# A two-layer graph network on one core: where the weight loads and the weight preparation stand among the operations of the first graphs

## The chip, the cores and the metric

The kernel runs on one core of a Trainium2 chip. The metric is the device time of one execution, in microseconds (us), as the median of several runs. A core has five engines, each with its own stream of instructions that it takes strictly in program order: PE (matrix multiply, with its weight loads shown as PEld), DVE (VectorE), ACT (ScalarE), POOL (GpSimd) and SP (SyncE), which here issues every transfer (DMA) between memory and the core. An engine that meets an instruction whose input is not there waits, and everything behind it on that engine waits too.

## What is computed

There are 64 graphs of 256 nodes with 256 features, and an adjacency matrix for each. Each graph goes through two layers:

```python
# layer 0: attention over 8 heads, with a value matrix chosen by the edge type
q, k = src @ Wq + bq, src @ Wk + bk
attn = softmax(q @ k.T / sqrt(dh))
out = sum over r of (attn * (adj == r)) @ (src @ Wv[r] + bv[r])
x = ln(src + out @ Wo + bo)                    # gain g1, shift beta1
x = ln(x + gelu(x @ W1 + b1) @ W2 + b2)        # gain g2, shift beta2
# layer 1: two graph attentions, then a feed-forward
h = gat(gat(x, adj, W1, a1), adj, W2, a2)      # the layer's own W1, W2
h = ln(x + h)
y = ln(h + relu(h @ w_ff1 + b_ff1) @ w_ff2 + b_ff2)
```

The weights are the same for all graphs. They are loaded once, and some are changed once before use (see below).

## The kernel before

**One plan, sorted.** The kernel writes its order out by hand. Each graph is an object whose `operations()` (line 697) gives 210 named operations: `xT` transposes the input on DVE, `qk0` and `qk1` are the query and key products on PE, `s0` and `s1` the scores, `maxmh`, `expmh`, `recmh`, `nrmmh` the softmax of head h in half m, `eTmh` its transpose in 32x32 squares on DVE, `eWmh` and `eRmh` the two transfers that finish that transpose by way of memory, `pmmh` the product with the mask, `po0` and `po1` the products with the values, `vp1` to `vp7` the value products and `va..` their sums, `wo` the output product; then the first feed-forward (`a..`, tiles ffa), the two graph attentions (`ga..`, `z..`, `h1..`, `h2`), the second feed-forward (`b..`, tiles ffb) and `store`. `load` brings in the input x (`xin`, four transfers) and the adjacency (`adi`) of one graph, `y` the input once more as a residual.

`PLACES` (line 29) gives each operation a number, its place. Operation n of graph g has the place `g * PERIOD + PLACES[n]` with `PERIOD` = 46.8, so some five graphs are under way at once. Places are only sorted; they are not waited for. The sorted list is the program order of all five engines:

```python
plan = [(t, len(PLACES), lambda i=i: nc.sync.dma_start(*loads[i])) for i, t in enumerate(LOAD_PLACES)]
for place, f in (
        (V_PLACE, v_weights),
        (OUT_PLACE, out_bias),
...
    plan.append((place, len(PLACES), f))
for g in range(B):
...
    plan += [(g * PERIOD + t, i, ops[n]) for i, (n, t) in enumerate(PLACES.items())]
with tc.manual_schedule():
    for _, _, f in sorted(plan, key=lambda p: p[:2]):
        f()
```

**Ahead of the plan** (lines 190 to 210) SP issues the input of graph 0 (`xin` in four transfers, `adi`), `wq`, `wk`, `bq_c`, `bk_c`, four blocks of `wv`, two rows of `bv_r` and `bv_c`, and DVE scales the query bias (`bqs_c`, line 210).

**In the plan** stand, beside the operations, 49 weight loads (`LOAD_PLACES`, in the order in which the list `loads` is filled, lines 213 to 239; the trace puts them all at line 791) and six steps that run once:

- `v_weights` (line 267), at `V_PLACE`: nine DVE instructions on `wv` and `bv_r`, which make the seven combined value matrices that `vp1` to `vp7` use.
- `out_bias` (line 275), at `OUT_PLACE`: four matmuls of `bv_c` with `wo` on PE (tile `bo_ps`), then one DVE addition into `bo_r`, which `yb` adds to the residual.
- `ffn_weights` (line 241), at `FFA_PLACE` for `w1`, `w2` and at `FFB_PLACE` for `f1`, `f2`: 32 matmuls with one output column on PE (line 247), two scalings of 128x1024 on ACT (line 251), and on DVE one small addition, one of 128x256 and four of 128x512 (lines 249, 252, 261 to 264).
- `gat_weights` (line 282), at `GAT_PLACE`: transposes and products on PE with DVE copies between them, each waiting for the one before (lines 289, 290, 297, 299, 304, 306), ending in `gext`, which `ga0` and `ga1` use.
- `any_odd` at `ODD_PLACE`, after the last graph's checks.

With the places before, the sorted list begins with 13 loads, `v_weights`, seven loads, `out_bias`, and 21 more loads. Only then come `te` of graph 0, one more load, and the first operations of graph 0: `xT`, `qk0`, `qkc0`, `chk`. The load of `bo_r`, which `out_bias` adds to, is the eighteenth of the plan's loads. The other seven loads are part 0 of `f1` behind the input load of graph 1, then `gl1_r`, a part of `gw1`, `bf2_r`, `bl2_r`, `be2_r` and `g2_r`, one at a time, among the operations of graphs 0 to 2. `ffn_weights` for `f1` stands just ahead of `xS` of graph 1 and the one for `w1` just ahead of `s1` of graph 1.

Of the kernel before, what the change touches and what calls it, by code (L numbers as in the profile page):

```python
# [63 lines left out]
    "rt4": 345.1762, "nb4": 348.7424, "ln4": 355.9706, "lg4": 361.3841, "lb4": 362.9841, "store": 364.6106,  # L64
}
LOAD_PLACES = [
    -1614.873, -876.860, -2013.345, -937.005, -414.952, -1429.108, -1287.906, -564.689, -101.489, -232.236, -554.653,
    -886.559, -645.093, -1037.230, -879.521, -1583.499, -310.508, -761.901, -160.300, 256.504, 211.016, -1033.278,
    -110.148, -55.769, 172.714, -816.528, -200.307, -634.823, -786.173, -139.875, 168.880, -731.757, 150.912,
    -640.846, -119.211, -981.427, -22.481, -1384.415, -1320.156, -1310.193, -716.722, -1407.675, -1020.008, 74.666,  # L70
    -646.340, -542.109, 179.232, -895.390, 197.294,
]
V_PLACE, OUT_PLACE, FFA_PLACE, GAT_PLACE, FFB_PLACE, ODD_PLACE = -942.888, -786.173, 197.294, 224.563, 183.686, 240.000

# [971 lines left out]
```

## Time and profile before

| What | us |
|---|---|
| median of 3 runs | 3197.49 |
| lowest and highest of the runs | 3196.38, 3198.89 |
| the profiled execution's own time | 3196.43 |
| its span in the trace | 3194.6 |
| span from 140 to 3040: PE busy, of 2900 | 2867.19 |
| DVE busy there | 2234.91 |
| ACT busy there | 2192.56 |
| POOL busy there | 2077.52 |
| first 25 us of the span: PE busy | 2.07 |

The span is the trace's time from the first to the last instruction; the execution's own time is 1.8 us longer. From 140 us on PE is busy 99% of the time and the others 72% to 77%. The profile gives, for each stretch of time, the busy time of each engine and the granted clock of PE (1.00 is full speed, 0.50 half). Transfers are told by their issue on SP; the median time from issue to landing was 3.1 us for a part of `xin`, 3.0 us for an `eW`, 3.5 us for an `eR`, 3.5 us for `bo_r` and 7.4 us for the 1 MB of `w2`. A load's issue on SP took 0.42 to 0.69 us, mostly 0.60.

### The profile page before, as it was taken

To read this page: it belongs to the slowest core of one execution; us is meant where nothing else is said; L and a number is where in the kernel's file an instruction comes from. 1 tells how busy PE (TensorE), PEld (TensorE's weight loads), DVE (VectorE), ACT (ScalarE), POOL (GpSimd) and SP (SyncE) were. 2 spreads that over 40 slices of the span, in tenths; PEclk is the share of its full clock that TensorE was granted. 3 is DMA by queue.
4 is the path that set the end of the run, shared out by engine and by line. 5 is a ranking of instruction groups with operands and counts; after the bars stand their busy time and mean duration, and the time that the engine had idled before them with its cause. 6 is when DMAs were issued, how large, how long until landed. Compare 5 with 4: busy or idle time off the path is not lost. (4 is left out here: it accounts for less than half of the span.)

```text
span 3194.6 us, 63709 instructions
## 1 busy us (share of the span) xinstructions
PE 3075.6 (96%) x21725; PEld 2586.6 (81%) x21725; DVE 2374.0 (74%) x5153; ACT 2325.6 (73%) x6599; POOL 2193.0 (69%) x2630
## 2 busy tenths in 40 slices
PE   6899999999999999999999999999999999999995
PEld 4688888888888888888888888888888888888774
DVE  5777777777777777777877877877777777777742
ACT  5677777777777777777777777777777777777742
POOL 1476776776776676676676676676677677677664
PEclk8999999999999999999999999999999999999997
DMA  6554455455455455455455455455455455455421
GB/s 194 148 151 144 141 154 146 139 154 149 138 152 150 140 149 152 140 148 154 137 150 154 136 151 154 137 151 153 136 151 152 137 151 151 138 153 150 133 70 31
DMA packets 808331, 456.62 MB, mean 143 GB/s; under 512 B 334528, under 2 KB 717376, under 8 KB 808000
## 3 DMA queue, kind: packets, MB, share of 16 engines
q1 hardware_dynamic: 808000, 452.49, 49.0%
q8 instruction: 174, 2.85, 0.4%
q14 instruction: 157, 1.29, 0.1%
HBM read 242.63 MB, written 201.33 MB: 139 GB/s over the span
## 5 line engine op out<-in xcount | busy, mean ns | idle before, releaser
L568 ACT ACTIVATE e<-e,rden 128x256 f32<-128x256 f32 x1024 | 455.9, 505 | 86.2 <-DVE rden L563 86.0
L408 PE MATMUL ffb_ps<-ffb_T,f 128*128 128x256 f32 x2048 | 461.7, 384 | 25.8 <-DMA ffb_T<-ffb_T_d 23.5
L408 PE MATMUL ffa_ps<-ffa_T,w 128*128 128x256 f32 x2048 | 474.6, 380 | 0.0
L558 ACT ACTIVATE e<-s,nmax 128x256 f32<-128x256 f32 x1024 | 469.3, 469 | 6.8 <-DVE nmax L550 3.8
L408 PEld LDWEIGHTS ffb_ps<-ffb_T,f 128*128 128x128 f32 x2048 | 392.6, 193 | 85.3 <-DMA ffb_T<-ffb_T_d 20.5
L577 DVE TENSOR_TENSOR pm<-eT,adT 128x512 f32<-128x512 f32 x512 | 437.7, 856 | 0.0
L326 DVE STREAM_TRANSPOSE eT_sq<-e 128x512 f32<-128x512 f32 x512 | 350.9, 695 | 110.7 <-DMA ffa_T_d<-ffa_T_sq 98.1
L408 PEld LDWEIGHTS ffa_ps<-ffa_T,w 128*128 128x128 f32 x2048 | 380.7, 191 | 47.4 <-ACT ffa_h L416 0.2
L373 POOL TENSOR_SCALAR rs_x<-mv_x 128x2 f32<-128x2 f32 x256 | 56.6, 221 | 453.1 <-DVE mv_x L369 445.6
L550 DVE TENSOR_REDUCE nmax<-s 128x2 f32<-128x512 f32 x512 | 336.0, 667 | 7.3 <-PE s L545 7.2
L416 ACT ACTIVATE ffb_h<-ffb_ps,bf_c 128x256 f32<-128x256 f32 x512 | 215.0, 472 | 123.4 <-PE ffb_ps L408 123.4
L384 ACT ACTIVATE ffa_res<-ffa_res,nb_x,rs_x 128x256 f32<-128x256 f32 x256 | 139.4, 594 | 191.5 <-POOL nb_x L379 185.3
L644 DVE SCALAR_TENSOR_TENSOR ga_z<-ga_z 128x512 f32<-128x512 f32 x64 | 88.1, 1377 | 235.9 <-ACT ga_z L641 235.9
L431 POOL TENSOR_TENSOR ffa_t<-ffa_h,ffa_t 128x512 f32<-128x512 f32 x128 | 165.1, 1290 | 128.8 <-ACT spare L692 121.5
L431 POOL TENSOR_TENSOR ffb_t<-ffb_h,ffb_t 128x512 f32<-128x512 f32 x128 | 191.0, 1492 | 89.2 <-ACT ffb_h L416 89.2
L416 ACT ACTIVATE ffa_h<-ffa_ps,b_c 128x256 f32<-128x256 f32 x512 | 214.3, 472 | 51.9 <-PE ffa_ps L408 51.1
L644 DVE SCALAR_TENSOR_TENSOR gb_z<-gb_z 128x512 f32<-128x512 f32 x64 | 44.3, 692 | 226.8 <-ACT gb_z L641 226.8
L558 ACT ACTIVATION_READ_ACCUMULATOR e<-s,nmax 128x1 f32 x1024 | 209.5, 205 | 0.0
L374 POOL TENSOR_TENSOR rs_x<-rs_x,nhalf 128x2 f32<-128x2 f32 x256 | 181.8, 710 | 21.3
L530 DVE TENSOR_TENSOR v<-v,v_ps 128x256 f32<-128x256 f32 x448 | 169.2, 400 | 0.6 <-PE v_ps L521 0.6
L351 POOL TENSOR_TENSOR ffa_res<-ffa_res,g_r 128x512 f32<-128x512 f32 x64 | 81.7, 1276 | 122.2 <-ACT ffa_res L384 122.2
L545 PE MATMUL s<-kT,qT 32*128 32x256 f32 x2048 | 149.9, 404 | 4.7 <-ACT e L558 4.7
(163 smaller groups left out, 8016.0 us busy)
## 6 DMA issues: line engine op xcount, KB each, us to landing
eT_d<-eT_sq SPq DMA_DIRECT2D x512, 256.0 KB, 3.0
eT<-eT_d SPq DMA_DIRECT2D x512, 256.0 KB, 3.5
xin<-in_x_dram SPq DMA_DIRECT2D x256, 64.0 KB, 3.1
adi<-in_adj_dram SPq DMA_DIRECT2D x64, 256.0 KB, 2.8
y<-in_x_dram SPq DMA_DIRECT2D x64, 256.0 KB, 4.4
ffa_T_d<-ffa_T_sq SPq DMA_DIRECT2D x64, 256.0 KB, 2.5
ffa_T<-ffa_T_d SPq DMA_DIRECT2D x64, 256.0 KB, 3.0
hT_d<-hT_sq SPq DMA_DIRECT2D x64, 256.0 KB, 2.0
```

The source lines that it names most:

```text
L326: nc.vector.transpose(self.sq.rearrange("p a c k y -> p (c k) a y"), src.rearrange("p c (k a x) -> p (c k) a x", k=KD, a=A))
L374: nc.gpsimd.tensor_tensor(self.rs, self.rs, nhalf, ALU.pow)
L384: nc.scalar.activation(yc, yc, AF.Identity, bias=self.nb[:, c:c + 1], scale=self.rs[:, c:c + 1])
L408: nc.tensor.matmul(p[:, f - f0, :], self.wa[:, k, f * P:(f + 1) * P], self.x.nodes(k), start=(k == 0), stop=(k == KD - 1))
L416: nc.scalar.activation(self.h[half][:, f1 + f, :], self.ps[f0][:, f, :], self.func, bias=self.ba[:, f0 + f:f0 + f + 1])
L431: nc.gpsimd.tensor_tensor(out, a, b, ALU.subtract)
L530: nc.vector.tensor_tensor(self.v_part(*to), self.v_part(*src), self.ps["v", i], ALU.add)
L545: nc.tensor.matmul(self.s4[m][h][:, ic * N:(ic + 1) * N], self.qT[hp, m, ic * P:(ic + 1) * P], self.kT[hp, m, :], start=True, stop=True)
L550: nc.vector.tensor_reduce(self.nmax[m, h], self.s4[m][h].rearrange("p (c n) -> p c n", c=C), AX.X, ALU.max, negate=True)
L558: nc.scalar.activation(e[:, ic, :], self.s4[m][h][:, ic * N:(ic + 1) * N], AF.Exp, bias=self.nmax[m, h][:, ic:ic + 1], accum_out=self.den[ ...
L568: nc.scalar.activation(e[:, ic, :], e[:, ic, :], AF.Copy, scale=self.rden[m, h][:, ic:ic + 1])
L577: nc.vector.tensor_tensor(self.pm[m, h].rearrange("p c k (b y) -> p (c k) b y", b=A), t.rearrange("p b c k y -> p (c k) b y"), self.adT.re ...
```

## The change

Only numbers change: the 49 places of `LOAD_PLACES` and five of the six places of the steps that run once. `PLACES` and every function stay as they are, so the order of the graphs' own operations among each other is the same.

```diff
 LOAD_PLACES = [
-    -1614.873, -876.860, -2013.345, -937.005, -414.952, -1429.108, -1287.906, -564.689, -101.489, -232.236, -554.653,
...
+    101.366, 142.216, 210.928, 179.882, 111.464, 161.951, 112.848, 100.995, 176.282, 144.653, 176.020, 153.991,
+    122.933, 161.019, 117.691, 142.137, 176.282, 109.079, 176.294, 241.513, 253.083, 121.392, 182.287, 196.253,
+    207.821, 129.075, 215.004, 184.114, 158.647, 204.480, 111.464, 207.869, 213.180, 214.956, 213.949, 222.383,
+    259.685, 196.355, 250.874, 266.888, 159.287, 109.005, 208.310, 182.294, 221.373, 230.689, 234.043, 257.548,
+    184.117,
 ]
-V_PLACE, OUT_PLACE, FFA_PLACE, GAT_PLACE, FFB_PLACE, ODD_PLACE = -942.888, -786.173, 197.294, 224.563, 183.686, 240.000
+V_PLACE, OUT_PLACE, FFA_PLACE, GAT_PLACE, FFB_PLACE, ODD_PLACE = 113.801, 158.647, 184.117, 225.125, 272.083, 240.000
```

Sorted, the plan then runs as follows (gN. is an operation of graph N; operations between those named are left out):

```
g0.te, w1 part 3, wo, g0.load, g1.te, g0.xT, bl1_c part 0, w2, w1 part 0, gl1_r, w1 part 2, V_WEIGHTS,
g0.qk0, be1_c 1, g0.qkc0, g0.chk, gw1 0, g1_c 3, g0.qk1 ... g0.max01, gx ... be1_c 2, bo_r, g0.cast, g1_c 0, g0.eT00 ...
g1.load, g0.s1 ... g0.eW00, g1_c 2 ... g1.xT, g0.vp1 ... g0.eW03 ... a part of gx, OUT_BIAS, g0.vc1, gl1_c 3 ...
g0.vp6, g0.y, be1_c 0, g1.qk0, w1 part 1, g0.eR03, g0.jT, g0.eW01 ... g0.eW10 ... g0.eR00, g0.eT02 ...
g1_c 1, b1_c, be1_c 3, b2_r, g0.eW02 ... g0.eR01, be1_r ... gw1 1, bl1_c 2, a2c 1, bl2_r, FFN_WEIGHTS(w1), g1.xS, g0.eW12 ...
g0.eR02, g0.eW11 ... g0.pm00, gw1 2, gl1_c 0, g0.eR12, g2.load, g1.s1, g0.po0 ... g2.xT ... a part of gx ...
gw1 3, g1.y, bl1_r ... bl1_c 1, g1.eR03, g1.jT, g0.pm13, g1_r, g1.eW01 ... f1 0, f1 2 ... f1 1, a2c 0 ... g1.eW10 ...
bl1_c 3 ... g1.eR00 ... f1 3 ... g0.aW, g1.eW02, g2.exp01, g2.max03, g1.yb, GAT_WEIGHTS, g2.rec00 ...
g0.aR ... f2, g2.xS, g1.eW12, g0.au3 ... bf2_r ... g2_r ... gl1_c 1 ... be2_r ... gl2_r ... bf1_c ...
g0.hT ... gl1_c 2 ... g0.hW ... g0.hR ... g2.yb, FFN_WEIGHTS(f1), g0.ga1, g0.gac1, g0.ga0 ...
```

Fourteen loads now stand ahead of `g1.load` (42 before) and 35 behind it (seven before). `GAT_PLACE` moves past `g2.exp01`, `g2.max03` and `g1.yb`. `FFB_PLACE` moves from the operations of graph 1 to the first graph attention of graph 0, behind all loads.

## The prediction, made before the changed kernel was run

> **What bounds the kernel now.** I read the page first, for the bound and for where the bound fails to hold; then windows of ten microseconds over the start; then the order of time and the waits there.
>
> ```profile
> span 3194.6 us, 63709 instructions
> PE 3075.6 (96%) x21725; PEld 2586.6 (81%) x21725; DVE 2374.0 (74%) x5153; ACT 2325.6 (73%) x6599; POOL 2193.0 (69%) x2630
> PE   6899999999999999999999999999999999999995
> PEclk8999999999999999999999999999999999999997
> ```
>
> PE is full in all slices but the first two and the last, and its clock is full there. So the time is the filling, then PE's work at full speed, then the draining. The change leaves all instructions and, behind the steps it moves, their order; it can only shift the moment from which PE stays full. The windows (PE, PEld, DVE, ACT and POOL busy, PE's granted clock, DMA share, GB/s) find that moment:
>
> ```profile
> 0.00:10.00 10.00, 0.00 (x0) 0.00 (x0) 0.55 (x4) 1.69 (x3) 0.69 (x6) 1.00 0.64 158
> 10.00:20.00 10.00, 2.07 (x4) 1.17 (x4) 2.73 (x8) 0.00 (x0) 0.00 (x0) 1.00 0.57 158
> 60.00:70.00 10.00, 9.28 (x65) 5.91 (x65) 9.86 (x21) 9.96 (x19) 0.00 (x0) 0.60 0.88 240
> 120.00:130.00 10.00, 5.59 (x31) 3.98 (x30) 8.24 (x20) 6.35 (x21) 9.59 (x15) 0.80 0.51 136
> 140.00:150.00 10.00, 10.00 (x93) 7.69 (x94) 4.95 (x8) 8.22 (x23) 5.04 (x4) 1.00 0.45 131
> ```
>
> PE does nothing of the graphs for 25 us, then is held up, and is full from 140 on. Up to there every microsecond by which the order of work comes forward comes off the end; behind it only added PE work counts. The order of time (start, duration, instruction, idle time before it and its releaser) shows what holds the start:
>
> ```profile
> 8.87 0.17 DVE L210 TENSOR_SCALAR bqs_c<-bq_c 128x2 f32<-128x2 f32 x1 [7.98 <-DMA bq_c<-in_L_gnn_bq_dram]
> 20.36 0.58 SPq L791 DMA_DIRECT2D bo_r<-in_L_gnn_bo_dram  x1
> 23.90 0.42 DVE L280 TENSOR_TENSOR bo_r<-bo_ps,bo_r 128x256 f32<-128x256 f32 x1 [9.42 <-DMA bo_r<-in_L_gnn_bo_dram]
> 24.24 0.70 DVE L468 STREAM_TRANSPOSE xT<-xin 128x512 f32<-128x512 f32 x1
> 38.99 2.64 SPq L185 DMA_DIRECT2D xin<-in_x_dram  x4
> 43.46 0.71 DVE L468 STREAM_TRANSPOSE xT<-xin 128x512 f32<-128x512 f32 x1 [2.16 <-DMA xin<-in_x_dram]
> 53.21 3.63 PE L247 MATMUL ffb_b_ps<-bl_c,f 128*128 128x1 f32 x32
> 54.51 0.71 DVE L326 STREAM_TRANSPOSE eT_sq<-e 128x512 f32<-128x512 f32 x1 [2.31 <-DMA eT_d<-eT_sq]
> 56.70 6.04 PE L247 MATMUL ffa_b_ps<-be_c,w 128*128 128x1 f32 x32
> 127.81 3.80 PE L622 MATMUL ga_wps<-gext,hT 128*128 128x260 f32 x8 [4.41 <-DMA hT<-hT_d]
> ```
>
> The first transpose stands on DVE behind the addition of `out_bias`, which waits for `bo_r`, eighteenth load of the plan. The input of graph 1 goes out at 38.99, behind 42 loads. From 54.5 to 77 DVE never idles, so DVE sets the pace there, while PE runs 58 to 67 at half speed.
>
> **The change, part by part**, in time against the profiled execution (3196.43; its span and 1.8 around it).
>
> *Start.* `xT` now follows `bqs_c` on DVE, which ends at 9.04. `xin` was issued by 3.52, and the slowest of its transfers took 5.2, so it is there by 8.7; `wq` and `wk` (issued 4.22, 4.74, landing in 3.8, 3.9) by 8.6. So `xT` starts at 9.1 instead of 24.24: **-15.2**. `v_weights` (nine DVE instructions) goes behind it, still waits for `bv_r` until 12.46 and ends at 14.5; `chk` ends at 15.1, and the next DVE work, the first maximum, comes at 32.52 - 15.2 = 17.3. It costs nothing; without that cover, 3.5 (4x0.29, 0.43, 4x0.42, less overlap).
>
> *Graph 1's input.* Fourteen loads stand ahead of it: 9.75 + 14x0.6 = 18.2. One more delay shows in SP's waits: of `w2` (1 MB, issued 21.97, 7.4 to land) the eighth next load waited 2.0 until 29.4. `w2` now goes out at 11.9 and the eighth next, `be1_c` 2, waits until 19.3, by which the issue comes to about 20.6; landed, 20.6 + 2.64 + 3.1 = 26.3. DVE is ready for it at 41.3 - 15.2 = 26.1. The wait of 2.16 goes; what I keep is **-1.0** (between 0 and -2.2), since `out_bias` now takes its 2.07 on PE there, in a gap that was 1.74 wide.
>
> *SP ahead of DVE.* The wait of 2.31 at 54.51 is for an `eW` that SP issued late: at 43 SP was still at the loads, so `eR03` and the adjacency transposes ran late. SP now comes to `eW00` at 24 (19 earlier), six loads more use up some 3 of its 4 us lead, and four of the later ones lie where SP would wait for `eT02` anyhow: **-2.0** (0 to -3.4, with the 1.14 wait before it).
>
> *ffn_weights.* Both stood at 53 to 69; now that of `w1` alone stands where that of `f1` stood. DVE, which sets the pace, loses 0.12 + 0.40 + 4x0.69 = 3.3 us of work, in the row from 59.81 to 62.84: **-3.0** (0 to -3.6). ACT loses 2.2, PE 3.6 to 6.0, none on the path. Its last inputs are near: `be1_c` 3 lands at about 38, when PE arrives at 37 to 38; `be1_r` at 42.5, DVE at 42: within the next term.
>
> *SP with more loads.* Between `y` of graph 0 and the step 11 loads stand against three, between graph 2's input and `wo` nine against one. I carried SP's queue forward by rows: graph 2's input lands about 1.0 behind DVE, and `eR13` brings `pm13` 1.2 late: **+2.2**. Bounds: nothing, if SP's own waits (31 us in the first 320 for DVE's value sums alone) take them up; 28 loads x 0.6 = +16.8 if none does.
>
> *gat_weights.* Its first DVE copy (86.07) now stands behind one more maximum: **+0.7**, since PE and DVE take turns in it (0 to +0.7).
>
> *ffn_weights for f1, new place.* It falls into PE's gap of 4.41 ahead of `ga1`, waiting for `hT`: 32 matmuls at 113 ns are 3.6. ACT was idle 2.63 there (needs 2.3); DVE then waits 3.53 for `ga_z` (needs 3.3). Cover gone, it is PE's 3.6; I take **+0.5**. The 1 MB of `f2` (5.6 to land) goes ahead of `eW12`; what needs the next `eR` comes 8 us later, so nothing (up to +5.6).
>
> One rule speaks for more. The Trainium skill, TensorE: Matmul & The Clock Gate, section "Why this matters for your kernels", asks for no idle gap of over some 3 us, as the clock falls by half after it; the gap at 123.4 agrees (0.50 from 126 to 132), and by the rule filling it would keep the clock. But the row of 56.70 shows 32 such matmuls back to back, with the clock at 0.50 from 58 on: one-column matmuls did not hold it. So I take nothing for the clock, and leave the rule's result a rival.
>
> Sum: -15.2 - 1.0 - 2.0 - 3.0 + 2.2 + 0.7 + 0.5 = **-17.8**, so 3178.6 for an execution like the profiled one; the median lies 1.1 higher: **3179.7**.
>
> **The rivals.**
>
> *The filled gap keeps the clock.* `ga_wps` then takes 8x0.24 = 1.9 instead of 3.8 (0.24: half of 0.475), and the 0.5 falls away: 3177.3. Against it stands the row at 56.70. With the skill's page beside it I give it 0.12. It shares this end with the case that SP costs nothing.
>
> *The loads cost half of what they can.* SP is one queue, and each head needs an `eW` and an `eR` from it. For it: DVE's waits in the first 320 us for writes that SP had issued late (7.1 on `ffa_T`, 3.6 on `eT_sq`). Half of 16.8 in place of 2.2 is 6.2 more, and half of the -2.0 is lost: 3179.7 + 7.2 = 3187. Chance 0.18.
>
> *The filling is bound by transfers.* Then an earlier start runs into the same bytes, and the time stays: 3196. For it: DMA share of 0.94 at 25 to 30 and 0.95 at 65 to 70. Against it: 0.35 and 0.14 at 115 to 125, and 0.64, 0.57 in the first 20 us. Chance 0.10.
>
> *SP decides (slower).* If all 28 loads push `eW` and `eR` out, 16.8, DVE's masks and so `po0`, `po1` come late by it, from the 11 loads ahead of `eW12` on; PE then idles over three times more, and each time pays what it paid at 123.4: clock 0.50 for 6.6 us, 3.3 lost, together 9.9. The gains of 2.0 and 1.0 go. 16.8 + 9.9 - 15.2 - 3.0 + 1.2 = +9.7: 3207. Against it: SP idles between 78 and 86 and between 89 and 96. Chance 0.07. A rule points that way: the Trainium skill, DMA: Bandwidth & Descriptors, "Rules for kernel authors", says to issue a transfer early and wait late. By the rows the early issue is what fills SP until 38.99; I follow the rows.
>
> **Chances and range.** Forecast 0.53 (own range 3174 to 3185), then 0.12, 0.18, 0.10, 0.07 in the order above. A change of 0.2% (6.4 us) is about what the measurement can tell from none. Faster by more: 0.53 + 0.12 + 0.18 = 0.83; within: 0.10; slower: 0.07. The range goes from 3171 (all lower ends: -15.2 - 2.2 - 3.4 - 3.6 - 1.9 = -26.3) to 3191, which takes in the half-cost case.
>
> **What would show it.** `xT` of graph 0 at 9.1 and first `qk_ps` at 9.8; graph 1's `xin` issued near 20.6 and its `xT` near 26.3; no wait for `eT_d` of over 1 us at `eT02`; DVE without ffb rows near 43; PE's 32 ffb matmuls ahead of `ga_wps`, which starts near 127.8 - 18 = 110; PE full from about 122. From there the stages should take what they took: one graph in about 47.7 (its `xin` at 608.5, then 656.3). The prediction is wrong if `xT` waits for something else, or if PE idles longer before 122 on `eR` or `xin` than before.

## The result, and the profile after

The changed kernel takes 3185.81 us (median of 6 runs, 3182.16 to 3187.17) against 3197.53 for the kernel before on the same chip (6 runs, 3194.36 to 3198.89). The ratio is 0.9962, with a 95% interval of 0.995 to 0.9975: 11.7 us faster, 0.4%. The profiled spans differ by nearly the same, 3194.6 and 3183.7. The forecast was 17.8 faster. The time lies within the whole range that was given (3171 to 3191), just outside the forecast's own (3174 to 3185), and nearer to the rival in which the loads cost half of what they can (3187).

The page of the changed kernel, its span, PE's busy time and granted clock in 40 slices:

```profile
span 3183.7 us, 63717 instructions
...
PE   6999999999999999999999999999999999999995
...
PEclk8999999999999999999999999999999999999997
```

Only the span and the second slice of PE (9 for 8) differ. All of the gain is in the first 150 us, as the windows show (PE, PEld, DVE, ACT and POOL busy, PE's clock, DMA share, GB/s):

```profile
10.00:20.00 10.00, 6.26 (x32) 4.08 (x30) 5.87 (x14) 4.83 (x17) 0.00 (x0) 0.98 0.87 258
...
120.00:130.00 10.00, 6.44 (x27) 4.86 (x26) 6.54 (x15) 8.57 (x24) 0.88 (x1) 0.94 0.68 184
130.00:140.00 10.00, 10.00 (x93) 7.95 (x92) 5.92 (x11) 5.96 (x17) 4.14 (x4) 0.89 0.34 103
```

PE works 6.26 us between 10 and 20, where it had 2.07 before. But it still has a hole between 120 and 130, at the time where the prediction wanted it to be full. The order of time of the changed kernel (start, duration, engine, line, instruction, idle time before it and its releaser) has most of the instructions that the prediction quoted of the kernel before, and three more:

```profile
5.67 0.71 DVE L468 STREAM_TRANSPOSE xT<-xin 128x512 f32<-128x512 f32 x1 [4.78 <-DMA xin<-in_x_dram]
7.60 2.04 PE L497 MATMUL qk_ps<-xT,wq 128*128 128x256 f32 x4 [7.60 <-DMA wq<-in_L_gnn_Wq_dram]
8.58 0.28 DVE L210 TENSOR_SCALAR bqs_c<-bq_c 128x2 f32<-128x2 f32 x1 [2.20 <-DMA bq_c<-in_L_gnn_bq_dram]
21.14 2.65 SPq L185 DMA_DIRECT2D xin<-in_x_dram  x4
25.76 0.71 DVE L468 STREAM_TRANSPOSE xT<-xin 128x512 f32<-128x512 f32 x1 [1.51 <-DMA xin<-in_x_dram]
35.92 0.71 DVE L326 STREAM_TRANSPOSE eT_sq<-e 128x512 f32<-128x512 f32 x1 [1.89 <-DMA eT_d<-eT_sq]
39.88 6.86 PE L247 MATMUL ffa_b_ps<-be_c,w 128*128 128x1 f32 x32 [4.68 <-DMA b_r<-in_L_gnn_b_dram]
46.77 0.17 DVE L249 TENSOR_TENSOR b_c<-ffa_b_ps,b_c 128x8 f32<-128x8 f32 x1 [4.32 <-PE ffa_b_ps L247]
108.97 4.37 PE L247 MATMUL ffb_b_ps<-bl_c,f 128*128 128x1 f32 x32
113.43 3.80 PE L622 MATMUL ga_wps<-gext,hT 128*128 128x260 f32 x8
127.24 2.90 PE L669 MATMUL h_ps<-ga_wh,ga_z 128*128 128x258 f32 x8 [3.56 <-ACT ga_wh L664]
```

The reader is to see three things. The head comes some 18 us forward (`xT`, `qk_ps` and the issue of graph 1's `xin`), and the addition of `out_bias`, which held it up, now stands at 27.63, behind the `xT` of graph 1. Two preparations then have a price that they had not before: the one for `w1` starts at 39.88, after PE has waited 4.68 us, and the one for `f1` at 108.97, behind which `h_ps` is late. And the wait of about 2 us at `eT02` (35.92) is still there.

To read off where time comes and goes, take the same instruction in both traces; the difference of the two starts is the lead at that point, and the change of the lead from one row to the next is what the work between them cost or gave.

| Instruction | before | after | lead |
|---|---|---|---|
| `xT` of graph 0, DVE | 24.24 | 5.67 | -18.6 |
| first `qk_ps`, PE | 25.00 | 7.60 | -17.4 |
| `xT` of graph 1 | 43.46 | 25.76 | -17.7 |
| `eT02` of graph 0 | 54.51 | 35.92 | -18.6 |
| `eT11` of graph 0 | 59.17 | 41.74 | -17.4 |
| `pm00` of graph 0 | 65.44 | 52.44 | -13.0 |
| `xT` of graph 2 | 70.89 | 54.83 | -16.1 |
| `wo` of graph 0, PE | 77.97 | 62.69 | -15.3 |
| `gext_ps`, PE | 89.13 | 75.08 | -14.1 |
| `wo` of graph 1 | 117.22 | 102.95 | -14.3 |
| `ga_wps` of graph 0 | 127.81 | 113.43 | -14.4 |
| first `gb_ips`, PE | 143.72 | 132.75 | -11.0 |
| `wo` of graph 4 | 256.48 | 245.54 | -10.9 |

From there to the last graph the lead at `wo` stays between 10.4 and 11.0: the later graphs run as they did.

### The profile page after: what moved, and what is told of

Its sections match the earlier page's. It is cut to its first block, busy times and chain, and to the rows that moved or that the text cites. A ratio compares the mean times of both kernels' runs of the same rounds, so it can differ in the third digit from the quotient of the medians.

```text
span 3183.7 us, 63717 instructions
## 1 busy us (share of the span) xinstructions
PE 3076.2 (97%) x21725; PEld 2588.3 (81%) x21725; DVE 2377.3 (75%) x5153; ACT 2328.3 (73%) x6599; POOL 2196.3 (69%) x2630
## 5 line engine op out<-in xcount | busy, mean ns | idle before, releaser
L408 PEld LDWEIGHTS ffb_ps<-ffb_T,f 128*128 128x128 f32 x2048 | 392.8, 193 | 84.7 <-DMA ffb_T<-ffb_T_d 20.6
```

The costliest lines, as they stand in the source:

```text
L408: nc.tensor.matmul(p[:, f - f0, :], self.wa[:, k, f * P:(f + 1) * P], self.x.nodes(k), start=(k == 0), stop=(k == KD - 1))
```

## The experiments

Each was run beside the kernel before on one chip, with five runs where no other number is given. "Lead" is used as above. Line numbers from the middle of the file on are four higher in the kernels with `ffn_seven`.

**Is it `bo_r` alone?** The kernel before, with `out_bias` alone at its new place.

```diff
-V_PLACE, OUT_PLACE, FFA_PLACE, GAT_PLACE, FFB_PLACE, ODD_PLACE = -942.888, -786.173, 197.294, 224.563, 183.686, 240.000
+V_PLACE, OUT_PLACE, FFA_PLACE, GAT_PLACE, FFB_PLACE, ODD_PLACE = -942.888, 158.647, 197.294, 224.563, 183.686, 240.000
```

> The kernel before with one place changed: out_bias at 158.647, as in the changed kernel; all loads stay ahead. If the wait of out_bias for bo_r was what held the start, the first transpose starts by 9.1 and the time falls by some 15, to about 3182. If SP's queue of 42 loads in front of graph 1's input holds the start just as much (my theory), the first transpose and graph 0's scores come 15 to 18 earlier, but graph 1's xin is issued at about 39 and transposed at 43 to 44 as before, and the time changes by 0 to -2: 3195 to 3198.

Measured: 3196.2 (3193.16 to 3199.39, 11 runs) against 3196.86; ratio 0.9999 (0.999 to 1.0008). Graph 0's `xT` came at 14.93, 9.3 earlier and not the 15 to 18 that were expected, since `v_weights` still stood ahead of it on DVE until 14.9. Graph 1's `xT` did not come earlier:

```profile
14.93 0.70 DVE L468 STREAM_TRANSPOSE xT<-xin 128x512 f32<-128x512 f32 x1
...
44.10 0.71 DVE L468 STREAM_TRANSPOSE xT<-xin 128x512 f32<-128x512 f32 x1 [12.58 <-DMA xin<-in_x_dram]
```

DVE saved 9.3 us and spent 12.58 waiting for graph 1's input, which SP still issued behind 42 loads. So the forward step on DVE was worth nothing here by itself; the queue on SP is the other half of the start.

**Is it the places of the loads or those of the steps?** The changed kernel, with its steps where they are and the 35 later loads all put back ahead of graph 1's input.

```diff
 LOAD_PLACES = [
-    101.366, 142.216, 210.928, 179.882, 111.464, 161.951, 112.848, 100.995, 176.282, 144.653, 176.020, 153.991,
...
+    101.366, 142.216, 149.900, 149.900, 111.464, 149.900, 112.848, 100.995, 149.900, 144.653, 149.900, 149.900,
...
```

> The changed kernel with its five steps where they are and all 35 later loads put back ahead of graph 1's input. It parts the loads from the steps. My theory, that SP's queue holds the start: graph 1's xin is issued near 42, its transpose comes near 46, 20 later than in the changed kernel, and what is gained by the places of the steps (one ffn_weights fewer on DVE, no wait for b1_c and be1_c) is 0 to 3: 3194 to 3199. The rival, that the places of the steps make the gain and SP has room for the loads anywhere: 3184 to 3187 as in the changed kernel.

Measured: 3199.11 (3196.13 to 3202.14, 11 runs) against 3196.61; ratio 1.0006 (0.9997 to 1.0015). The order of time:

```profile
42.22 3.18 SPq L185 DMA_DIRECT2D xin<-in_x_dram  x4
...
49.06 0.71 DVE L468 STREAM_TRANSPOSE xT<-xin 128x512 f32<-128x512 f32 x1 [24.55 <-DMA xin<-in_x_dram]
```

The whole lead of graph 0 (18.7 at its `xT`) becomes one wait of 24.55. Together the two runs show that the new places of the steps give nothing while the loads stand ahead of the second graph's input. The other half, the loads moved and `out_bias` left ahead of graph 0, was not run. That it would give nothing either is only argued: `bo_r` went out at 19.83 in the changed kernel, 0.5 earlier than before, and graph 0's `xT` would go on waiting for it.

**Were five late loads the price of the preparation for `w1`?** In the changed kernel, the loads that `ffn_weights` of `w1` needs last (`be1_c` 3, `b1_c`, `be1_r`, `b2_r`, and `g1_c` 1) change places with five earlier loads that nothing needs so soon.

```diff
-    101.366, 142.216, 210.928, 179.882, 111.464, 161.951, 112.848, 100.995, 176.282, 144.653, 176.020, 153.991,
...
+    101.366, 142.216, 210.928, 121.392, 111.464, 161.951, 112.848, 100.995, 111.464, 144.653, 159.287, 153.991,
...
```

> The changed kernel with five pairs of loads swapped, the number of loads at each point of SP's queue unchanged: be1_c part 3, b1_c, be1_r, b2_r and g1_c part 1, which ffn_weights of w1 needs, take the early places of bl1_c part 0, gl1_r, a part of gw1, gx and gl1_c part 3. If the late landing of be1_c part 3 costs the changed kernel what it seems to (PE waits 4.7 for it, its clock falls, DVE waits 4.3), PE's 32 matmuls start near 35 and take 3.6, DVE's wait of 4.3 goes, and the time falls by about 4.3, from 3185.8 to 3181.5. The rival: the next wait takes its place (graph 2's input, or eR12 and eR13, which SP issues no earlier), and 1 to 2 are left: 3184.

Measured: 3184.82 (3181.31 to 3185.66); ratio 0.9959 (0.9945 to 0.9972), no difference from the changed kernel that the runs can tell, as the rival has it. The order of time (PE's row first, then DVE's):

```profile
35.59 3.63 PE L247 MATMUL ffa_b_ps<-be_c,w 128*128 128x1 f32 x32
...
37.26 0.71 DVE L326 STREAM_TRANSPOSE eT_sq<-e 128x512 f32<-128x512 f32 x1 [2.69 <-DMA eT_d<-eT_sq]
...
57.29 0.69 DVE L577 TENSOR_TENSOR pm<-eT,adT 128x512 f32<-128x512 f32 x1 [1.95 <-DMA eT<-eT_d]
```

The step itself was mended as meant: PE began at 35.59 without a wait, took 3.63 instead of 6.86, and DVE no longer waited for it. But the lead, 18.1 at graph 2's `xT`, was 14.0 at `wo` of graph 0, 1.3 less than without the swap. Waits for `eT_d` and `eT` took its place, all of them for transfers that SP issues. The reading is that SP as a whole was late there and that the five loads were only where it first showed; the run that takes thirteen loads away (below) tests it.

**Does the preparation for `f1` hold up the first graph attention?** The last five DVE instructions of that step move to place 291.0, behind `zlA` to `h10`; its matmuls, scalings and first addition stay.

```diff
             nc.scalar.activation(w[:, k], w[:, k], AF.Copy, scale=gain[:, k])
+        if name == "ffa":
+            ffn_seven(row, shift_row, name, wb, wb_t)
+
+    def ffn_seven(row, shift_row, name, wb, wb_t):
         nc.vector.tensor_tensor(row, row, shift_row, ALU.add)
...
+            (291.0, lambda: ffn_seven(bf2_r, bl1_r, "ffb", f2, f2_t)),
```

> The changed kernel with ffn_weights of f1 cut in two: its matmuls, the small addition and ACT's scalings stay at 272.083; the addition of 128x256 and the four of 128x512 on DVE move to 291.0, ahead of graph 0's second score step, where DVE waits 7.4. If DVE's 5.9 us there (1.6 for single additions of 128x512 that took 0.7 elsewhere) delay graph 0's first attention and so PE's h_ps, h_ps starts 1.7 earlier, PE's clock does not fall behind it, and the time falls by 1.7 to 3.4, to 3182.4 to 3184.1. The rival, that PE's 32 matmuls and the half clock behind them cost it: no change, 3185.8.

Measured: 3182.26 (3179.81 to 3183.8); ratio 0.9954 (0.9941 to 0.9968). Against its own runs of the kernel before that is 14.6 faster, where the changed kernel was 11.7 faster; the intervals overlap, and the trace places the difference: the lead, 13.7 at `ga_wps` (0.7 less than in the changed kernel), is 13.8 at `gb_ips` and stays so, while the changed kernel fell from 14.4 to 11.0 there. First the rows in question in the changed kernel, DVE's and POOL's order of time together:

```profile
113.46 0.84 DVE L252 TENSOR_TENSOR bf_r<-bf_r,shifts 128x256 f32<-128x256 f32 x1
...
114.85 1.71 POOL L351 TENSOR_TENSOR ffa_res<-y,g_r 128x512 f32<-128x512 f32 x1
115.47 1.64 DVE L262 TENSOR_TENSOR f_t<-f_t,f 128x512 f32<-128x512 f32 x1
116.63 1.59 POOL L354 TENSOR_TENSOR ffa_res<-ffa_res,b_r 128x512 f32<-128x512 f32 x1
117.14 1.64 DVE L263 TENSOR_TENSOR f_t<-f,f_t 128x512 f32<-128x512 f32 x1
```

The same instructions in the kernel of this experiment, and PE's `h_ps` there:

```profile
115.28 1.26 POOL L355 TENSOR_TENSOR ffa_res<-y,g_r 128x512 f32<-128x512 f32 x1
...
125.48 0.42 DVE L256 TENSOR_TENSOR bf_r<-bf_r,shifts 128x256 f32<-128x256 f32 x1
...
126.12 2.26 PE L673 MATMUL h_ps<-ga_wh,ga_z 128*128 128x258 f32 x8 [1.94 <-ACT ga_wh L668]
126.53 0.69 DVE L266 TENSOR_TENSOR f_t<-f_t,f 128x512 f32<-128x512 f32 x1
```

And `h_ps` in the kernel before:

```profile
139.90 2.26 PE L669 MATMUL h_ps<-ga_wh,ga_z 128*128 128x258 f32 x8 [1.85 <-ACT ga_wh L664]
```

Apart, both engines are quick: 0.69 and 1.26. Together, DVE takes 1.64 and POOL 1.6 to 1.7 for the same shapes. With the first row at 0.84 instead of 0.42, the step took DVE from 113.38 to 119.30 (5.9 us) instead of 3.1 to 3.3, `zlA` began at 121.18 instead of 119.97, and PE's wait ahead of `h_ps` was 3.56 instead of 1.94. Against the 1.85 of the kernel before, the longer wait is half of the 3.4 that was lost. The other half is PE's clock behind the wait: from `h_ps` to `gb_ips` PE took 5.5 us in the changed kernel, with the granted clock at 0.50 from 129 to 132, and 3.8 in this one and in the kernel before. The 5.5 stands in all three kernels that have the whole step at its new place (the changed one, the one with the swaps, the one with all loads ahead), with waits of 2.74 to 3.56 ahead of `h_ps`; the 3.8 stands in four of the five with the step cut in two, and their waits are 1.67 to 1.94. So the shorter wait goes with the cut in every one of these traces, the full clock only in most.

**Both mends together.** The five swaps and the split.

```diff
-    101.366, 142.216, 210.928, 179.882, 111.464, 161.951, 112.848, 100.995, 176.282, 144.653, 176.020, 153.991,
...
+    101.366, 142.216, 210.928, 121.392, 111.464, 161.951, 112.848, 100.995, 111.464, 144.653, 159.287, 153.991,
...
+            (291.0, lambda: ffn_seven(bf2_r, bl1_r, "ffb", f2, f2_t)),
```

> Both edits, the swapped loads and the cut step. If the two costs are separate and stand one behind the other, the gains add: -6.0 to -7.7, 3178.1 to 3179.8. If they share a wait, no more than the larger: 3181.5.

Measured: 3181.96 (3179.43 to 3184.77); ratio 0.9957 (0.9943 to 0.997). The median is near the 3181.5 of a shared wait, but its times cannot be told from those of the split alone, nor from the sum of both gains. Its trace has a lead of 15.5 at the end against 13.8, but up to place 272 this program is the one with the swaps alone, whose trace had graph 2's `xT` 2.1 later. So 2 us between two single traces is within what one program shows from run to run, and this one settles nothing about the swaps.

**Take loads out of SP's way.** From the kernel with both mends, thirteen loads that lay ahead of `wo` of graph 0 or just behind it (`f1`, `bl1_c`, two parts of `gl1_c`, and three rows) go behind it.

```diff
-    207.821, 176.294, 215.004, 184.114, 158.647, 204.480, 176.282, 207.869, 213.180, 214.956, 213.949, 222.383,
-    259.685, 196.355, 250.874, 266.888, 176.020, 176.282, 208.310, 182.294, 221.373, 230.689, 234.043, 257.548,
-    184.117,
+    207.821, 176.294, 215.004, 184.114, 158.647, 204.480, 300.000, 257.548, 236.950, 236.950, 236.950, 236.950,
+    259.685, 250.874, 250.874, 266.888, 250.874, 236.950, 236.950, 236.950, 236.950, 230.689, 234.043, 257.548,
+    300.000,
```

> The kernel with both edits (3182.0; span 3177.6), with 13 loads that only ffn_weights of f1 and later steps need moved out of the stretch in which graphs 0 and 1 need SP: the parts of f1 and of bl1_c to a place where SP was idle for 5 us (between eR02 and eW11 of graph 1), the others later. If the loads in SP's queue are what took back the gain of the swap (graph 2's xin at 46, eR13 late for pm13, po1 waiting 2.7 for it), xin of graph 2 goes out 2 to 3 earlier, po1's wait goes, and the time falls by 2 to 4, to 3178 to 3180. The rival, that DVE and the round trip of each transfer hold this stretch: no change.

Measured: 3180.86 (3178.47 to 3181.9); ratio 0.9948 (0.9935 to 0.9962). What was expected of the stretch came about: graph 2's `xin` went out at 43.26 instead of 46.04, `po1` waited 0.80 instead of 2.74, and the lead at `wo` of graph 0 is 19.7, where it was 16.0. The time did not follow: it is above the expected 3178 to 3180 and cannot be told from the run before, and at `wo` of graph 1 the lead is 15.2, where it was 14.8. The loads had only been moved to another place where SP was the last to come, as the next two kernels show.

**`gat_weights` put back.** The same, with `GAT_PLACE` as in the kernel before.

```diff
-V_PLACE, OUT_PLACE, FFA_PLACE, GAT_PLACE, FFB_PLACE, ODD_PLACE = 113.801, 158.647, 184.117, 225.125, 272.083, 240.000
+V_PLACE, OUT_PLACE, FFA_PLACE, GAT_PLACE, FFB_PLACE, ODD_PLACE = 113.801, 158.647, 184.117, 224.563, 272.083, 240.000
```

> The same as the run with the 13 loads moved, and GAT_PLACE back at 224.563, ahead of graph 2's max03. The prediction's term for that move was +0.7, so a fall of 0.7: too little for the time, but the products of graph 0's first feed-forward on PE start 0.6 to 0.7 earlier behind the start of gat_weights. The rival, that DVE's maximum fits into a wait: no difference between the two.

Measured: 3180.47 (3175.84 to 3184.27); ratio 0.9948 (0.9934 to 0.9962). The times do not tell the two apart. In the traces the lead is alike at `wo` of graph 0 (19.6 and 19.7), and 19.6 instead of 18.2 at `gext_ps`, so by these two traces the move cost 1.4 there; at `wo` of graph 1 it is 15.0, as without it. SP's order of time in this kernel shows who takes the lead back:

```profile
71.98 3.32 SPq L795 DMA_DIRECT2D f<-in_L_gnn_w_ff_dram  x4
77.06 2.54 SPq L795 DMA_DIRECT2D bl_c<-in_L_gnn_b_ln_dram  x4
...
81.47 3.07 SPq L185 DMA_DIRECT2D xin<-in_x_dram  x4
```

Graph 3's input goes out at 81.47, behind eight loads; DVE waited 3.12 for it at 87.64, and PE 4.03 at 94.91 for what DVE had behind it. Yet SP had issued nothing from 60.98 to 66.23, while it waited for `aT`.

**The eight loads into that gap.** The last kernel moves them from 236.95 to 223.5, just ahead of `aW` of graph 0.

```diff
-    207.821, 176.294, 215.004, 184.114, 158.647, 204.480, 300.000, 257.548, 236.950, 236.950, 236.950, 236.950,
-    259.685, 250.874, 250.874, 266.888, 250.874, 236.950, 236.950, 236.950, 236.950, 230.689, 234.043, 257.548,
+    207.821, 176.294, 215.004, 184.114, 158.647, 204.480, 300.000, 257.548, 223.500, 223.500, 223.500, 223.500,
+    259.685, 250.874, 250.874, 266.888, 250.874, 223.500, 223.500, 223.500, 223.500, 230.689, 234.043, 257.548,
```

> The kernel of e6 with one move: the eight loads that stood ahead of graph 1's eW11 and graph 3's input (f1 parts 0 to 3 and bl1_c parts 0 to 3, place 236.95, issued 71.98 to 79.60 there) go to place 223.5, just ahead of graph 0's aW, where SP stood idle from 60.98 to 66.23 in e6. Theory (the loads on SP took back the lead of 3 us between wo of graph 0 and wo of graph 1, because they held back eW11 and graph 3's input): eW11 and graph 3's xin go out 2 to 4 us earlier than the 79.70 and 81.47 of e6, the wait of DVE for that xin shrinks from 3 to under 1, wo of graph 1 comes 2 to 3 earlier than the 102.18 of e6, and wo of graph 3 lies 18 to 19 ahead of the kernel before instead of 16.2; time 3176 to 3179. Rival (the lead is taken by the order of DVE's and PE's own work, or by what stands next in the queue, and SP's loads only show it): wo of graph 1 within 1 us of e6 and the time 3179 to 3182. If the loads hold back aW of graph 0 instead, au0 of graph 0 comes later than the 73.12 of e6.

Measured: 3177.4 (3173.59 to 3178.03, 5 runs) against 3195.85; ratio 0.9937 (0.9924 to 0.9951). SP's order of time:

```profile
61.35 2.58 SPq L795 DMA_DIRECT2D f<-in_L_gnn_w_ff_dram  x4
63.98 2.54 SPq L795 DMA_DIRECT2D bl_c<-in_L_gnn_b_ln_dram  x4
66.61 0.54 SPq L335 DMA_DIRECT2D ffa_T_d<-ffa_T_sq  x1
...
77.60 3.23 SPq L185 DMA_DIRECT2D xin<-in_x_dram  x4
```

The eight issues fill the gap, `aW` still goes out at 66.61, and graph 3's input is 3.87 earlier. DVE has no wait ahead of graph 3's `xT` any more, `wo` of graph 1 has a lead of 19.4, and 18.5 of it arrive at the end. `eW11` of graph 1 goes out 3.4 earlier, and `au0` of graph 0 does not come later (73.10 against 73.12). So the theory holds and the rival falls; one number was too small, as `wo` of graph 1 came 4.4 earlier and not 2 to 3. This is the fastest version, 18.5 us ahead of the kernel before and some 7 ahead of the changed one (their intervals just touch).

## Why the gain was smaller than forecast

The direction and the main mechanism were right: the lead is won in the head, nothing changes in the later stages, and most of what happens between is SP's queue. Two terms of the sum were far too small, the one for SP's loads and the one for the step of `f1`. The terms are set against the rows of the table above; they come from one trace each, so differences of under 2 us between them are not settled:

- **Start**, forecast -15.2: measured -17.4. The term took `xT` to stand behind `bqs_c`. In the changed program it stands ahead of it (5.67 and 8.58), and the first `qk_ps` then waits for `wq` until 7.60. `xin` and `wq` also landed earlier than the 8.7 and 8.6 that were taken: the 5.2 in that sum is the slowest of all 256 transfers of `xin`, and graph 0's four took 2.4 to 3.8 in the kernel before, 2.4 to 2.7 in the changed one.
- **Graph 1's input**, forecast -1.0: -0.3 (the lead goes from 17.4 to 17.7). The issue at 21.14 was forecast at 20.6, `xT` at 25.76 at 26.3. Since DVE was ready at 24.25 and not at 26.1, it still waited 1.51.
- **SP ahead of DVE**, forecast -2.0: -0.9. This step fails as put: "no wait for `eT_d` of over 1 us at `eT02`" was to be seen, and the wait is 1.89. SP did come 18 us earlier, but it then met `y`, two loads and the adjacency transposes (30.10, 2.58 long) while DVE had come forward by as much.
- **SP with more loads**, forecast +2.2: +6.4, the term that is most wrong. It is the sum of 1.2 at `eT11`, which waits 1.08 for a transfer that stood behind four loads; 4.4 up to `pm00`, the preparation for `w1` that PE began 4.68 late and at half speed; and 0.8 in waits for `eT` up to `wo`. The prediction had set `be1_c` 3 to land at about 38 with PE arriving at 37 to 38. It was issued at 36.36, and PE, ready at 35.2, could start at 39.88 only (the profile names `b_r` there, the load right behind, which these matmuls do not read). The swaps show that this load was not the cause by itself, since other transfers from SP were late in its stead. Taking thirteen loads away, with the swaps kept, gives a lead at `wo` of graph 0 of 19.3 to 19.7 in three traces, against 14.0 to 16.0 in the four traces that leave the loads there, with the swaps or without; and the last kernel kept nearly all of that to the end. So the price was SP's queue as a whole. That is the mechanism of the rival of half cost, which had 8.4 for this term. That its time of 3187 came so near is in part luck: this term was 2.0 smaller than it had, the start gave 2.2 more, and the step for `f1` took 2.9 more, which it had not seen.
- **ffn_weights, one fewer at 53 to 69**, forecast -3.0: -3.07, from the lead before and behind graph 2's `xT` (13.0 to 16.1). DVE had one wait of 0.24 at 57.89 in the stretch where the prediction has it never idle; the term does not change by it.
- **gat_weights**, forecast +0.7: +1.2 from `wo` to `gext_ps`, which putting it back returned as 1.4.
- **ffn_weights for `f1`**, forecast +0.5: +3.4 (14.4 to 11.0). PE's 4.37 us did fall in the gap, and `ga_wps` kept its lead. The step that failed is "DVE then waits 3.53 for `ga_z` (needs 3.3)": the 3.3 was measured while POOL was idle, and took 5.9 beside POOL. Of the 3.4, 1.7 is the longer wait ahead of `h_ps` (3.56 against 1.85) and 1.7 the half clock behind it, for which the prediction took nothing. Moving the five instructions away gave all of it back in four of the five kernels, and the wait alone in the last.

The terms measured come to -17.4 - 0.3 - 0.9 + 6.4 - 3.1 + 1.2 + 3.4 = -10.7, and 0.3 more came on the way from `gext_ps` to `ga_wps` (14.1 to 14.4): -11.0.

**The rivals.** That the filled gap keeps the clock falls: `ga_wps` took 3.80 in both kernels, with the granted clock at 0.50 between 113 and 118 although PE was busy with the 32 one-column matmuls right ahead and had no wait between. The clock fell while they ran: it was 1.00 from 110 to 111 and 0.50 from 112 on. The Trainium skill, TensorE: Matmul & The Clock Gate, "Why this matters for your kernels", asks for no idle gap over some 3 us between matmuls. There was none here, and by that rule alone `ga_wps` would have taken 1.9, an estimate of half its 3.80; the row decides. That transfers bind the filling falls: the changed kernel moves the same bytes and is 11.7 us faster, and the last one is 18.5 us faster. That SP decides for a slower kernel did not come about; with all loads ahead of graph 1's input SP took the whole gain, but no more than that (ratio 1.0006).

## What to carry to other kernels

An issue of some 0.6 us on a queue costs nothing where that queue idles (the eight in the last kernel) and its full time where it is the next to be late (35 loads put graph 1's input from 21.14 to 42.22); so look for the issuing queue's own idle stretches and put loads there, instead of "early" or "late". After a mend, compare the lead at several instructions along the trace: a lead that is back to its old value 40 us later has met another wait, here one of the same queue. And take the duration of a step that is moved from rows in which its new neighbours were running.

## What the runs showed of the hardware

DVE and POOL slow each other. The four DVE instructions from 113.46 to 118.78 take 0.40 + 0.68 + 0.69 + 0.69 = 2.46 us with POOL idle (the kernel before, 59.86 to 62.3), and POOL's three additions and products beside them 0.72 + 1.26 + 1.26 = 3.24 (the split kernel). One after the other they would need 5.70; together they took 5.3. The trace of the kernel with all loads ahead shows the same durations again (0.83, 1.64 and 1.64 on DVE, 1.72 and 1.59 on POOL). Transfers are not the reason: the DMA share was 0.76 between 113 and 119 here and 0.78 in the kernel before between 59.8 and 62.9, where DVE took 0.69. The Trainium skill, SBUF — State Buffer, "Who interferes with whom", says that a DVE instruction with two inputs in that memory contends with a POOL instruction that reads it; the rows agree.

PE's clock is not explained by the wait ahead of it alone. `h_ps` took 2.90 after a wait of 3.56 in the changed kernel and 2.26 after 1.94 in the split kernel, but 2.75 after the same 1.94 in the last one. No run settles what the clock goes by there. The last kernel still loses 1.7 us of its lead between `h_ps` and `gb_ips`.
